# First loads in written order, lora_B behind the last weight block, A in three transfers, and column steps at multiples of 16

## The chip, the cores and the metric

The kernel runs on one core of one Trainium2 chip. The metric is device time in microseconds: the median of three runs is 418.48 us before the change (417.75 to 418.6). Besides these there is one profiled execution, from which all durations in this text come.

## What is computed

For each of 64 batch entries a 64x64 matrix is picked from 16 by an index and applied to x; the result goes through a 1024x1024 layer and a routed rank-8 correction, and is added to x.

```python
W = weights[condition]                                   # one of 16, for each batch entry
c = jnp.einsum('bct,bcd->bdt', x, W).reshape(-1, 1024)   # 4096 rows
top1 = jnp.argmax(c @ gate_w.T + expert_bias, axis=-1)   # one of 4 experts
base = c @ W_up.T
z = jnp.einsum('nh,erh->ner', c, lora_A)                 # rank 8
d = jnp.einsum('ner,ehr->neh', z, lora_B)                # scale 1
out = x + base + (the row d[n, top1[n]])
```

All is float32, and x has 64 x 64 x 1024 elements.

## The kernel before

**Order of the algebra.** The picked matrix acts on the rows of a batch entry and the layer on its columns, so the kernel first multiplies x by one wide matrix (gate, lora_A and W_up side by side: `NW` = 1060 columns), giving `u`, and then applies the picked matrix (`bd`, block diagonal for two batch entries) to `u`. x is cut into 32 tiles of 128 rows, and two tiles form a group `g`. Each float32 operand is split into a high and a low part (`split_a`, `split_b`: ACT copies the rounded value, DVE subtracts it), and each product is three matmuls: high by high, high by low and low by high.

**Blocks.** A group's rows (tile a, tile b) and the contraction (two halves of four 128-row slices, `KH` = 4) give A11, A12, A21, A22; the wide matrix is cut in the same way into B11, B12 (columns 530 to 1059), B21 and B22. Each block of B is loaded in four slices k of 128 x 530 (265 KB) by `load_b`, into temporary buffers of a pool of ten. The first two groups (`eight`) compute all eight block products; the other fourteen (`seven`) compute seven products with sums of blocks, `S1` to `S4` and `T1` to `T4`. A product of 530 columns goes in two PSUM banks of 264 and 266 columns (`BANKS`, `CUT`).

**The start.** For the first group `load_halves` brings A11 and A21 together on ACT's queue, slice k=0 alone and k=1 to 3 in one transfer, and A12 with A22 on SP's. SP's queue also has all slices of B. TensorE's order in group 0 is: A11 and A21 by B11, slice by slice; A12 and A22 by B21; A11 by B12; A21 by B12; A12 by B22; A22 by B22. Small warm-up matmuls (`keep_warm`) stand before and between the first slices.

**What sets the order.** `InOrder` wraps an engine so that its instructions keep the order in which they are written; the lists of hooks (`at`, `each`) put the work of ACT, DVE and the queues behind a given slice of a given product. Loads given to `nc.sync` instead of the wrapped `sync` may be placed by the planner elsewhere in SP's queue. In the kernel before, `load_b`, `load_half`, the first B11 pieces, A12/A22 and lora_B are such loads; the planner put two of lora_B's three transfers (`load_b3`, 32 rows of 4 KB each) ahead of the last slice of B12, and the third behind B22. An SP load that shares a completion counter with the eighth load before it waits for that one to land; some wait for a temporary buffer too.

**ACT's order after the first products**, as far as it matters here: the four slices of B12, the first `bd`, B22's first slice, `u` of tile 0 (`uh`), B22's second, `u` of tile 1, lora_B (`split_b3`), `zt`, B22's last two.

**Columns of y.** Each tile's `u` is applied and written in three steps, `COLS`, of at most 354 columns. The first 36 columns are gate and lora_A, so the steps cover 318, 354 and 352 columns of y. `finish` is one step: `apply` (three matmuls with `bd`), `delta` (one with lora_B), `evict`. The last two tiles are written step by step. Tile 30 (`LAST`) has four steps, and the last product of its group is made one bank after the other (`product_by_bank`).

Of the kernel before, what the change touches and what calls it, by code (L numbers as in the profile page):

```python
# [17 lines left out]
KH = KC // 2  # L18
H = KC * P
E, R = 4, 8  # L20
ER = E * R
# [2 lines left out]
NB = NW // 2  # L24
CUT = 264
LEFT = 512 - CUT
COLS = ((0, 354), (354, 354), (708, 352))
LAST = ((0, 354), (354, NB - 354), (NB, CUT), (NB + CUT, NB - CUT))
WARM = 27
GATE = (("lg", E), ("mx", 1), ("sc", E), ("m2", 1), ("zm", ER))  # L30
HALVES = (slice(0, 64), slice(64, 128))
# [14 lines left out]
def kernel(  # L46
# [53 lines left out]

    def load_half(i, hf):
        t = raw[i, hf] = xp.tile([P, KH, P], F32, name="xh", tag="xh")
        nc.sync.dma_start(t, xt[i, hf])

    def minus_both(t, one, two):
        vector.scalar_tensor_tensor(t, one, -1.0, two, ALU.mult, ALU.subtract)
# [32 lines left out]
    def part(q, k):  # L139
        i, j = int(q[1]) - 1, int(q[2]) - 1  # L140
        return w[j][KH * i + k]

    def load_b(q, k):
        t = raw[q, k] = temp("wraw")
        nc.sync.dma_start(t, part(q, k))  # L145

    def split_b(q, k, n=slice(0, NB)):
        scalar.copy(wh[q][:, k, n], raw[q, k][:, n])
# [58 lines left out]
            )  # L207

    BANKS = slice(0, CUT), slice(CUT, NB)

    def product(g, which, hooks):

# [7 lines left out]

    def product_by_bank(g, places, a, b, hooks):

        for m, (o, n) in enumerate(zip(places, BANKS)):
            for k in range(KH):
                part_of_product(g, a, b, True, k, o[:, : n.stop - n.start], n)
                for kk, fn, *args in hooks:
                    if kk == KH * m + k:
                        fn(*args)
# [61 lines left out]
            vector.tensor_sub(b[p, 1, p], t[p], b[p, 0, p].bitcast(F32))  # L290

    FIRST = NB - G

    def place():
        return psum.tile([P, 512], F32, name="o", tag="o", bufs=2)
# [53 lines left out]
    def evict(i, j):  # L349

        s, d = ycols(i, j)
        o = os_.pop((i, j))[:, s]
        if i == NP - 1 or d.start >= FIRST and i == NP - 2:
            vector.tensor_add(ys[i][:, d], o, ys[i][:, d])
            sync.dma_start(out[i, :, d], ys[i][:, d])
            return
        if i < NP - 2 and j == 0:
            ys[i] = yp.tile([P, H], F32, name="y", tag="y")
        scalar.copy(ys[i][:, d], o)
        if i == NP - 2 and j == 1:  # L360
            n = slice(0, FIRST)
            pool.dma_start(ys[i][:, n], x[i][:, n], accum_op=ALU.add)
        elif j == 2:
            pool.dma_start(ys[i], x[i], accum_op=ALU.add)
            nc.sync.dma_start(out[i], ys.pop(i))
# [25 lines left out]
            raw["x", hf][:, :, k], xt[0:2, hf].rearrange("i p k q -> p i k q")[:, :, k]  # L391
        )

    ONE, REST = slice(0, 1), slice(1, KH)
    load_halves(scalar, 0, ONE)
    load_halves(scalar, 0, REST)

    one = cpool.tile([P, 1], F32, name="one")
    vector.memset(one, 0.0)
# [10 lines left out]
    t = raw["B11", 0] = temp("wraw")  # L410
    pieces = slice(0, CUT), slice(CUT, NB)
    for n in pieces:
        nc.sync.dma_start(t[:, n], part("B11", 0)[:, n])  # L413
    for k in range(1, KH):
        load_b("B11", k)
    load_halves(nc.sync, 1, slice(0, KH))
    for k in range(KH):
        load_b("B21", k)
    split_a(0, "A11", ONE)
    split_b("B11", 0, pieces[0])  # L420
    split_b("B11", 0, pieces[1])
    split_a(0, "A21", ONE)

    row = cpool.tile([P, 1], I32, name="row")
    for p in HALVES:
# [24 lines left out]
    def load_b3():  # L450
        b3f = yp.tile([3 * ER, H], F32, name="b3f", tag="y")
        for a in range(3):
            nc.sync.dma_start(b3f[ER * a : ER * a + ER], lb)
        raw["b3"] = b3f

    def split_b3():
# [19 lines left out]
    def eight(g):  # L476
        a, b = 2 * g, 2 * g + 1
        h = [[] for _ in range(6 if g == 0 else 8)]

        def at(s, k, fn, *args):  # L480
            h[s].append((k, fn, *args))

        def each(s, k, fn, q, ks, *args):
            for i in ks:
                at(s, k, fn, q, i, *args)

        one, two = (0, 1), (2, 3)
        if g == 0:
            each(0, -1, load_b, "B12", range(KH))
            at(0, 0, keep_warm, 6)  # L490
            at(0, 0, split_a, g, "A11", REST)
            at(0, 0, make_idx)
            for i in range(4):
                at(0, 0, load_cond, i)
            each(0, 0, split_b, "B11", (1,))
            at(0, 0, split_a, g, "A21", REST)
            each(0, 0, split_b, "B11", two)
            at(0, 1, keep_warm, 4)
            at(0, 0, split_a, g, "A12")
            each(0, 0, split_b, "B21", (0,))  # L500
            at(0, 1, split_a, g, "A22")
            each(0, 2, split_b, "B21", (1, 2))
            each(0, 3, split_b, "B21", (3,))
            each(1, -1, load_b, "B22", range(KH))
            at(1, 0, load_b3)
            for i in (2, 3):
                at(1, 0, load_half, i, 0)
            each(1, 0, split_b, "B12", (0,))
            each(1, 1, split_b, "B12", (1,))
            each(1, 2, split_b, "B12", two)  # L510
            at(1, 2, split_cond, a)
            at(1, 3, split_cond, b)
            each(1, 3, split_b, "B22", (0,))
            at(2, -1, lambda: u_of(a, 0, c["1"]))
            at(2, 0, load_two, 0)
            at(2, 0, load_two, 1)
            each(2, 0, split_b, "B22", (1,))
            at(2, 2, apply, a, 0)
            at(2, 2, gate, a)
            at(2, 2, lambda: u_of(b, 0, c["2"]))  # L520
            at(2, 3, split_b3)
            at(3, 1, turn, a)
            for i in (2, 3):
                at(3, 0, load_half, i, 1)
            each(3, 1, split_b, "B22", two)
            at(3, 2, split_a, g + 1, "A11")
            at(3, 3, delta, a, 0)
            at(3, 3, evict, a, 0)
            at(4, 1, apply, b, 0)
            at(4, 1, gate, b)  # L530
            at(4, 2, split_a, g + 1, "A21")
            at(5, -1, lambda: u_of(a, 1, c["3"]))
            at(5, 0, turn, b)
            at(5, 0, sum_t1, one)
            at(5, 0, load_two, 2)
            at(5, 0, load_two, 3)
            at(5, 2, delta, b, 0)
            at(5, 2, evict, b, 0)
            at(5, 2, end_t1, one)
            at(5, 3, split_a, g + 1, "A12")  # L540
            at(5, 3, finish, a, 1)
            order = (
                [("1", "A11", "B11", True), ("2", "A21", "B11", True)],
                [("1", "A12", "B21", False), ("2", "A22", "B21", False)],
                ("3", "A11", "B12", True),
                ("1", "A21", "B12", True),
                ("3", "A12", "B22", False),
                ("1", "A22", "B22", False),
            )
        else:  # L550
            p = a - 1
            at(0, -1, lambda: u_of(p, 1, cs[g - 1]["1"]))
            at(0, 1, finish, p - 1, 2)
            at(0, 1, split_a, g, "A22")
            at(0, 2, make_t1, two)
            at(0, 3, finish, p, 1)
            at(1, 0, finish, p, 2)
            at(1, 1, load_cond, a + 2)
            at(1, 1, load_cond, b + 2)
            for i in (b + 2, a + 2):  # L560
                at(1, 1, load_half, i, 0)
                at(2, 1, load_half, i, 1)
            at(2, 1, make_t2, one)
            at(3, -1, lambda: u_of(a, 1, c["1"]))
            at(3, 2, make_t2, two)
            at(4, -1, lambda: u_of(b, 1, c["2"]))
            at(4, 1, sums, g + 1, "S1")
            at(4, 2, split_cond, a)
            at(4, 2, split_cond, b)
            at(5, 0, sums, g + 1, "S2")  # L570
            at(5, 1, split_a, g + 1, "A11")
            at(5, 2, sums, g + 1, "S3")
            at(6, 0, split_a, g + 1, "S2")
            at(7, -1, lambda: u_of(a, 0, c["3"]))
            at(7, 0, sums, g + 1, "S4")
            order = (
                ("1", "A11", "B12", True),
                ("2", "A21", "B12", True),
                ("1", "A12", "B22", False),
                ("2", "A22", "B22", False),  # L580
                ("3", "A11", "B11", True),
                ("1", "A21", "B11", True),
                ("3", "A12", "B21", False),
                ("1", "A22", "B21", False),
            )
        run(g, order, h, c)
        cs[g] = dict(c)


    def seven(g):  # L590
# [6 lines left out]
        def at(s, k, fn, *args):  # L597
            h[s].append((k, fn, *args))
# [115 lines left out]
        if last:  # L714
# [8 lines left out]
            places = place(), place()  # L723

            def u_bank(m):
                n = BANKS[m]
                vector.tensor_add(s[:, n], places[m][:, : n.stop - n.start], ts["t8"][:, n])
                scalar.copy(us[a][0][:, NB + n.start : NB + n.stop], s[:, n])

            def u_bank_low(m):  # L730
                n = BANKS[m]
                u_low(a, slice(NB + n.start, NB + n.stop), s[:, n])

            product_by_bank(
# [8 lines left out]
                    (5, u_bank_low, 0),  # L743
                ],
            )
            sync.dma_start(out[a, :, :FIRST], ys[a][:, :FIRST])
            u_bank(1)
            finish(b, 2, chain()[:, :512])
            u_bank_low(1)
# [52 lines left out]
```

## Time and profile before

| | us |
|---|---|
| median of three runs | 418.48 |
| time of the profiled execution | 422.16 |
| its span, first to last instruction | 420.4 |
| TensorE busy | 410.9 |
| DVE busy | 285.5 |
| ACT busy | 184.6 |
| first matmul of a product | 4.19 |
| last matmul starts | 415.6 |

The page has one line of busy times by engine, a row for each engine in forty slices of the span (10.5 us each, a digit for tenths), the granted clock of TensorE in the same slices, the chain of work that ended last, and groups of like instructions. A line of the timeline has: start, duration, engine, line of the source, operation, output<-inputs, sizes, how many instructions were merged, and in brackets how long the engine stood idle before and what ended that. PE is TensorE, PEld its weight load, DVE the vector engine, ACT the scalar engine, POOL GpSimd, SP the engine that issues most transfers. Line L42 is the wrapper `InOrder`, so almost all instructions have it, and the names of tiles tell them apart: `hB`, `lB` are high and low of the B blocks, `hT`, `lT` those of T1 to T4 (B12 lives in T4's buffer and so shows as `hT`), `ah`, `al` those of A, `wraw` a loaded slice of B, `xx` the first A halves, `b3f` lora_B as loaded, `c` and `o` PSUM.

### The profile page before, as it was taken

The numbers are of one execution on the slowest core, as the hardware profiler recorded it, in microseconds if no ns is written. First come the engines' busy times: TensorE is split into PE (matmuls) and PEld (weight loads), VectorE is DVE, ScalarE is ACT, GpSimd is POOL, SyncE is SP. The second block draws the span as 40 slices with busy tenths as digits, with TensorE's granted clock in tenths as the row PEclk, the third lists the DMA queues.
The fourth block names the chain that finished last, engine by engine and source line by source line (L and its number), as shares of the span: only waits on it lengthen the run. The fifth ranks groups of instructions, "written<-read, shape, count | busy, mean of one in ns | idle before, by whom it ended". The sixth has DMA issues, their size and how long they took to land.

```text
span 420.4 us, 8155 instructions
## 1 busy us (share of the span) xinstructions
PE 410.9 (98%) x3197; PEld 408.7 (97%) x3197; DVE 285.5 (68%) x643; ACT 184.6 (44%) x416; POOL 75.8 (18%) x92
## 2 busy tenths in 40 slices
PE   8979999999999999999999999999999999999995
PEld 7969999999999999999999999999999999999995
DVE  4587784876766767676666757666676676666755
ACT  5564655353434534343353434445334444524531
POOL 6202611202020210202011020201102020020000
PEclk9989999999999999999999999999999999999998
DMA  8966992455654436564354655535464453564435
GB/s 274 317 227 175 225 248 54 111 166 134 175 120 84 132 106 177 133 154 101 95 145 120 175 133 133 123 81 152 127 177 133 102 125 93 165 170 113 90 63 175
DMA packets 25414, 60.99 MB, mean 145 GB/s; under 512 B 3264, under 2 KB 4928, under 8 KB 25376
## 3 DMA queue, kind: packets, MB, share of 16 engines
q1 hardware_dynamic: 18128, 40.74, 27.3%
q0 software_dynamic: 6704, 19.21, 26.9%
q8 instruction: 25, 0.41, 0.4%
q10 hardware_dynamic: 544, 0.52, 0.4%
q14 instruction: 13, 0.11, 0.1%
HBM read 43.68 MB, written 16.78 MB: 144 GB/s over the span
## 4 chain that ended last, share of the span: by engine, by line
PE 93%; DMA 4%; DVE 1%; SPq 0%; issue 0%; ACT 0%; DVEq 0%
PE c L42 77%; PE o L42 16%; DMA wraw<-in_w_dram 2%; DMA xx<-in_xt_dram 2%; SPq L145 0%; SPq L413 0%; DVE bd L42 0%; DVE ul L42 0%; DVE al L42 0%; ACT hT L42 0%; ACT ah L42 0%; DVE lB L42 0%; DVE y L42 0%; DVE lT L42 0%; DVEq L42 0%
## 5 line engine op out<-in xcount | busy, mean ns | idle before, releaser
L42 PE MATMUL c<-hT,ah 128*128 128x264 f32 x480 | 140.7, 293 | 0.0
L42 PE MATMUL c<-lT,ah 128*128 128x264 f32 x480 | 137.9, 287 | 0.0
L42 PE MATMUL c<-hT,al 128*128 128x264 f32 x480 | 137.9, 287 | 0.0
L42 PE MATMUL c<-hB,ah 128*128 128x264 f32 (+1 forms) x424 | 122.1, 288 | 0.6 <-ACT hB L42 0.5
L42 PE MATMUL c<-lB,ah 128*128 128x264 f32 (+1 forms) x424 | 121.0, 285 | 0.4 <-DVE lB L42 0.4
L42 PE MATMUL c<-hB,al 128*128 128x264 f32 (+1 forms) x424 | 121.0, 285 | 0.0
L42 PEld LDWEIGHTS c<-lT,ah 128*128 128x128 f32 x480 | 91.8, 191 | 0.0
L42 PEld LDWEIGHTS c<-hT,al 128*128 128x128 f32 x480 | 91.6, 191 | 0.0
L42 PEld LDWEIGHTS c<-hT,ah 128*128 128x128 f32 x480 | 91.6, 191 | 0.0
L42 POOL DMA_DIRECT2D y<-in_x_dram x31 | 29.8, 960 | 290.2 <-ACT y L42 285.2
L42 PEld LDWEIGHTS c<-lB,ah 128*128 128x128 f32 x424 | 80.5, 190 | 0.7 <-DVE lB L42 0.7
L42 PEld LDWEIGHTS c<-hB,ah 128*128 128x128 f32 x424 | 80.2, 189 | 1.0 <-ACT hB L42 1.0
L42 PEld LDWEIGHTS c<-hB,al 128*128 128x128 f32 x424 | 80.1, 189 | 0.0
L42 ACT COPY y<-o 128x318 f32<-128x318 f32 (+2 forms) x91 | 40.1, 442 | 58.2 <-PE o L42 56.3
L42 ACT CAST uh<-usum 128x530 fp32r<-128x530 f32 (+4 forms) x44 | 27.1, 616 | 69.7 <-DVE usum L42 69.7
L42 DVE TENSOR_TENSOR al<-S,ah 128x512 fp32r<-128x512 f32 x56 | 38.5, 687 | 24.2 <-ACT ah L42 24.2
L42 DVE TENSOR_TENSOR al<-xh,ah 128x512 fp32r<-128x512 f32 x46 | 31.7, 689 | 30.2 <-ACT ah L42 30.2
L42 PE MATMUL o<-uh,bd 128*128 128x354 f32 (+2 forms) x186 | 45.3, 325 | 2.7 <-ACT uh L42 2.7
L42 DVE TENSOR_TENSOR ul<-usum,uh 128x530 fp32r<-128x530 f32 (+4 forms) x44 | 30.0, 682 | 18.6 <-ACT uh L42 18.6
L42 ACT CAST zt<-o 96x128 fp32r<-96x128 f32 x31 | 8.1, 261 | 77.8 <-PE o L42 77.8
L42 POOL DMA_INDIRECT wsel<-in_cw_dram,idx x32 | 35.2, 1101 | 10.5 <-issue 5.2
L42 ACT CAST ah<-S 128x512 fp32r<-128x512 f32 x56 | 34.9, 623 | 1.8 <-DVE S L42 1.4
(87 smaller groups left out, 471.6 us busy)
## 6 DMA issues: line engine op xcount, KB each, us to landing
xh<-in_xt_dram SPq DMA_DIRECT2D x60, 256.0 KB, 5.1
y<-in_x_dram POOLq DMA_DIRECT2D x30, 512.0 KB, 5.7
out_dram<-y SPq DMA_DIRECT2D x30, 512.0 KB, 2.9
wraw<-in_w_dram SPq DMA_DIRECT2D x23, 265.0 KB, 7.2
T<-in_w_dram POOLq DMA_DIRECT2D x8, 265.0 KB, 6.7
xx<-in_xt_dram SPq DMA_DIRECT2D x1, 512.0 KB, 7.2
wsel<-in_cw_dram,idx POOLq DMA_INDIRECT x32, 5.0
y<-in_x_dram SPq DMA_DIRECT2D x1, 512.0 KB, 3.3
```

The lines of the kernel that those rows point to most:

```text
L42: return lambda *a, **k: self.tc.keep_in_program_order(fn(*a, **k))
```

## The change

- `load_b`, the first B11 pieces, A12/A22, lora_B and the x halves of the first four tiles go through the wrapped `sync`, in written order. lora_B's three transfers so stand behind B22.
- A11/A21 come in three transfers: k=0 and k=1 on ACT's queue, k=2 and 3 on SP's between B11's second and third slice. B11's second slice is split in two column pieces (264 and 266), as the first was, and A's splits follow the three transfers.
- Four warm-up matmuls instead of six after the first slice.
- `COLS` and `LAST` have new limits, so that the steps of y have 320, 352 and 352 columns. For tile 30 the last two steps have 258 and 272 instead of 264 and 266, and the banks of the last product follow (`LAST_BANKS`). The stores of tile 30 are cut at column 480 (`STORED`) instead of 494.

```diff
-COLS = ((0, 354), (354, 354), (708, 352))
-LAST = ((0, 354), (354, NB - 354), (NB, CUT), (NB + CUT, NB - CUT))
+COLS = ((0, 356), (356, 352), (708, 352))
+LAST = ((0, 356), (356, NB - 356), (NB, 258), (NB + 258, NB - 258))
...
-        nc.sync.dma_start(t, xt[i, hf])
+        (sync if i < 4 else nc.sync).dma_start(t, xt[i, hf])
...
-        nc.sync.dma_start(t, part(q, k))
+        sync.dma_start(t, part(q, k))
...
+    LAST_BANKS = [slice(c0 - NB, c0 - NB + n) for c0, n in LAST[2:]]
...
+    STORED = FIRST // 16 * 16
...
+            if d.start == FIRST:
+                d = slice(STORED, d.stop)
             sync.dma_start(out[i, :, d], ys[i][:, d])
...
-    ONE, REST = slice(0, 1), slice(1, KH)
-    load_halves(scalar, 0, ONE)
-    load_halves(scalar, 0, REST)
+    STEPS = slice(0, 1), slice(1, 2), slice(2, KH)
+    for k in STEPS[:2]:
+        load_halves(scalar, 0, k)
...
-        nc.sync.dma_start(t[:, n], part("B11", 0)[:, n])
-    for k in range(1, KH):
+        sync.dma_start(t[:, n], part("B11", 0)[:, n])
+    load_b("B11", 1)
+    load_halves(sync, 0, STEPS[2])
+    for k in range(2, KH):
         load_b("B11", k)
-    load_halves(nc.sync, 1, slice(0, KH))
+    load_halves(sync, 1, slice(0, KH))
...
-    split_a(0, "A11", ONE)
-    split_b("B11", 0, pieces[0])
-    split_b("B11", 0, pieces[1])
-    split_a(0, "A21", ONE)
+    def split_first(k):
+        split_a(0, "A11", STEPS[k])
+        for n in pieces:
+            split_b("B11", k, n)
+        split_a(0, "A21", STEPS[k])
+
+    split_first(0)
...
-            nc.sync.dma_start(b3f[ER * a : ER * a + ER], lb)
+            sync.dma_start(b3f[ER * a : ER * a + ER], lb)
...
-            at(0, 0, keep_warm, 6)
-            at(0, 0, split_a, g, "A11", REST)
+            at(0, 0, keep_warm, 4)
+            at(0, 0, split_first, 1)
...
-            each(0, 0, split_b, "B11", (1,))
-            at(0, 0, split_a, g, "A21", REST)
-            each(0, 0, split_b, "B11", two)
+            at(0, 0, split_a, g, "A11", STEPS[2])
+            each(0, 0, split_b, "B11", (2,))
+            at(0, 0, split_a, g, "A21", STEPS[2])
+            each(0, 0, split_b, "B11", (3,))
...
-            sync.dma_start(out[a, :, :FIRST], ys[a][:, :FIRST])
+            sync.dma_start(out[a, :, :STORED], ys[a][:, :STORED])
```

More of the change, by code (lines that the diff above doesn't have):

```diff
@@ L221, in product_by_bank @@
     def product_by_bank(g, places, a, b, hooks):
-        for m, (o, n) in enumerate(zip(places, BANKS)):
+        for m, (o, n) in enumerate(zip(places, LAST_BANKS)):
             for k in range(KH):
@@ L725, in u_bank @@
             def u_bank(m):
-                n = BANKS[m]
+                n = LAST_BANKS[m]
                 vector.tensor_add(s[:, n], places[m][:, : n.stop - n.start], ts["t8"][:, n])
@@ L730, in u_bank_low @@
             def u_bank_low(m):
-                n = BANKS[m]
+                n = LAST_BANKS[m]
                 u_low(a, slice(NB + n.start, NB + n.stop), s[:, n])
```

## The prediction

> **What bounds the kernel now.** I read the busy shares first, then TensorE's timeline, then the chain that ended last, then the stretches of the DMA engines. The first two lines are from the page.
>
> ```profile
> PE 410.9 (98%) x3197; PEld 408.7 (97%) x3197; DVE 285.5 (68%) x643; ACT 184.6 (44%) x416; POOL 75.8 (18%) x92
> ...
> PEclk9989999999999999999999999999999999999998
> ```
>
> TensorE is busy 98% of the span. In its timeline the starts of neighbouring matmuls lie 0.12 us apart, and from 28.4 us on no two lie more than 0.26 us apart until the last ones at 415 us. So nothing that another engine or a transfer does after 28.4 us sets the end; what can be won lies before it and behind 415.9 us, where TensorE stops. Its timeline before 28.4 us, in two pieces:
>
> ```profile
> 7.21 0.39 PE L42 MATMUL c<-hB,ah 128*128 128x264 f32 x1 [0.47 <-ACT hB L42]
> 7.95 0.40 PE L42 MATMUL c<-lB,ah 128*128 128x264 f32 x1 [0.36 <-DVE lB L42]
> ```
>
> ```profile
> 20.65 0.28 PE L42 MATMUL c<-hT,al 128*128 128x266 f32 x1
> 23.61 0.59 PE L42 MATMUL o<-uh,bd 128*128 128x354 f32 x2 [2.67 <-ACT uh L42]
> 24.49 0.43 PE L42 MATMUL o<-ul,bd 128*128 128x354 f32 x1 [0.29 <-DVE ul L42]
> ...
> 25.26 0.43 PE L42 MATMUL c<-hT,ah 128*128 128x266 f32 x1
> 25.48 0.43 PE L42 MATMUL c<-lT,ah 128*128 128x266 f32 x1
> ```
>
> There are two holes. The small one waits for the halves of the second B11 block. The large one stands after the third block of B12 and names ACT's `uh`; the chain that ended last and ACT's timeline tell why `uh` was late:
>
> ```profile
> 3.08 7.24 DMA xx<-in_xt_dram
> ...
> 11.71 9.09 DMA wraw<-in_w_dram
> ```
>
> ```profile
> 20.82 0.63 ACT L42 CAST hT<-wraw 128x530 fp32r<-128x530 f32 x1 [3.82 <-DMA wraw<-in_w_dram]
> ...
> 22.96 0.59 ACT L42 CAST uh<-c 128x530 fp32r<-128x530 f32 x1
> ```
>
> ACT sat in its queue for the fourth block of B12, issued at 11.71 and landed at 20.80 us. SP's timeline has two of lora_B's transfers ahead of it (issued 10.34 and 11.01), and the stretches show what happened to the DMA engines (busy us and matmuls, clock, DMA share, GB/s):
>
> ```profile
> 12.00:13.60 1.60, 1.60 (x15) 1.00 1.08 404
> 13.60:15.60 2.00, 2.00 (x18) 1.00 1.04 211
> 15.60:17.60 2.00, 2.00 (x19) 1.00 1.07 284
> ```
>
> The engines stay full while the rate falls by half for about 4 us. The third block of B12 landed at 16.3, the two pieces of lora_B at 17.5 and 18.3, then came 2.5 us until the fourth block, and after it one B22 block each 0.7 us.
>
> **The change, part by part.**
>
> *lora_B behind B22.* In SP's order the fourth block of B12 moves from behind two lora_B pieces to directly behind the third, and the four B22 blocks move up by two places. An SP load waits for the landing of the eighth transfer before it, so the fourth block may go at about 10.4 us (when A12/A22 has landed) instead of 11.71. At the 0.7 us per block seen after 20.8 it lands near 17, and the first B22 block, which ACT splits ahead of `uh`, near 18. TensorE needs them at 20.8. The hole then closes: from 20.77 (20.65 plus one interval of 0.12) to 24.76, where B12's fourth block starts, is 3.99 us, less the three real `o` matmuls in it at 0.16 each: **3.50 us** saved, if the loads come in before 19.
>
> *What follows the hole.* Of the matmuls from 25.04 to 28.36, fifteen are 0.221 us apart instead of 0.122: 15 x 0.099 = **1.5 us**, at a granted clock of 0.50 between 26 and 28 us. That row against a rule: the Trainium skill (TensorE: Matmul & The Clock Gate, Part 1: The HAM clock gate) says that an idle window of some 3.4 us halves the clock, and that the window runs freely, not from the start of the program. By the row the closed hole returns 1.5 us; by the rule it is a matter of where the windows fall, and an execution in which the hole straddles two windows never paid it, so there is nothing to return. I keep 1.5 for the profiled execution and **0.7** for the median; 0 and 1.5 are the ends.
>
> *A11 and A21 in three transfers.* Columns k=1 (128 KB) now come alone on ACT's queue; k=2 and 3 (256 KB) go to SP behind the second B11 block. That block landed at 6.46 with 384 KB of A beside it; with 256 KB less ahead, at the 0.33 MB/us of these stretches, it lands some 0.75 us sooner. ACT and DVE also split it in two pieces (0.41 and 0.43 us each instead of 0.63 and 0.71), so the first product can start after half of it. The k=1 products start near 6.6 instead of 7.21 and no longer wait 0.75 us for the low half: TensorE gets to the end of the step over a microsecond earlier. But there it meets A12/A22, which landed at 10.32: ACT 0.63, ACT 0.64, DVE 0.71 bring the first low half of B21 to 12.39, and TensorE came for it at 12.77. Only 0.38 us of slack is there, so of the 1.1 us I count **0.35**. Two warm-up matmuls less are inside this. A rule speaks against even that: DMA: Bandwidth & Descriptors, Issuing engines are not separate DMA queues, has all queues run on the same 16 engines, so that moving a transfer from ACT to SP buys nothing but the issue time (and here SP issues one more, 0.43 us). By the rule this part is 0, by the row 0.35; I follow the row, as B11's block really shared the engines with bytes not wanted yet. With A12/A22 landing 0.5 us late it would be -0.15, with it 0.8 sooner 1.1.
>
> *Loads in written order.* Loads of x halves of the first four tiles keep their places; B22's third and fourth wait for their buffers (DVE's low halves of B21, 12.4 and 13.6), as they did. The three lora_B pieces queue behind B22, ahead of the x halves and the reloaded B11/B12, whose places and bytes are unchanged. Queued behind lora_B on ACT: its split (1.05), `zt`, the splits of B22's last two blocks.
>
> *Columns.* 354+354+352 becomes 356+352+352, and 318+354+352 becomes 320+352+352: the same 1060 and 1024 columns, so TensorE's sum is unchanged: **0** for the body. In the last tile 264/266 becomes 258/272: six columns more in each of five last links, 0.03 us. The last stores become 240, 136 and 136 KB. The trace has 176 KB (352 columns, starting at a multiple of 16) landing in 2.4 us, 177 KB (354) in 2.6 and the very last 133 KB in 2.7; so 0 to 0.3 us, taken as **0.1**.
>
> *Sum.* In the profiled execution 3.5 + 1.5 + 0.35 + 0.1 = 5.45: its span goes from 420.4 to 414.95, its time from 422.16 to 416.7. That execution is 3.68 us above the median of the runs, and the page doesn't say where. For the median I take 3.5 + 0.7 + 0.35 + 0.1 = 4.65: **418.48 - 4.65 = 413.8 us**.
>
> **Rivals.** *The excess sits in the hole.* If the 3.68 us are all in the 5.0 us of hole and half clock, the plain runs have 1.3 of it to give, and with the two small terms 1.75: 416.7. For it: the rest of the kernel is paced by TensorE alone. Against: the dip to 211 GB/s is too deep to be the profiler's.
>
> *lora_B is late for the first correction.* The first product with lora_B (`o<-b,zt`) ran at 30.08; 5.35 us sooner is 24.7. Before it stand ACT's split 1.05, DVE's 1.22 and `zt`'s low half 0.3: the last piece must land by 22.1. Its bytes: 5.78 MB up to it in queue order, 4.08 moved by 13.6; 1.4 MB at 0.38 MB/us and the last 0.39 at 0.21 give 19.3, and 2 us from moved to landed, as for B21's last block, 21.3. If it still lands at 24.2, 2.1 us are lost again: 415.9.
>
> *The same, and worse: slower.* lora_B's transfers are the ones beside which the rate fell; now they run beside the x halves and reloads. Each us of landing past 22.1 costs one; the gain is gone at 26.75, and from 27.6 the kernel is slower by over 0.2%. At 28.5 it is 420.2. Against: that is 4 us later than it landed before with the same bytes ahead.
>
> *The dip belongs to the gathers of `wsel`* issued at 7.3 to 12.0, not to lora_B. Then the fourth block gains only the 256 KB, 0.7 us, and the clock stays as it was: with the small terms 1.15, 417.3.
>
> **How the numbers follow.** A change of 0.2% (0.84 us) is about what a measurement of this kernel tells from none. Chances: hole gone and most of its price back 0.59 (412.4 to 415.2), excess in the hole 0.18, lora_B late 0.10, gathers 0.07, slower 0.06. Low end of the range: 3.5 + 1.5 + 0.8 + 0.3 = 6.1, 412.4; high end 417.0, past the second and third case. Faster: 0.59 + 0.18 + 0.10 + a third of the gathers, 0.89; same 0.05; slower 0.06.
>
> **What would show it.** The step from B12's third to fourth block without a gap and ACT's wait for `wraw` before `hT` under 1 us; a granted clock of 1.00 from 24 to 30 us; B12's fourth block landing before 19; the k=1 products starting by 6.7 and B21's first still near 12.3; `o<-b,zt` first at 24.7 and unstalled; the stretch at 211 GB/s moved to about 17 to 20 us; TensorE's end at 410.5. I am wrong if a new hole stands ahead of `o<-b,zt`, if the rate still halves near 14 us, or if B21 waits for A12.

## The result, and the profile after

| us | before | after |
|---|---|---|
| median (16 runs each) | 418.57 | 416.83 |
| lowest to highest | 417.0 to 420.54 | 415.84 to 418.3 |
| profiled execution: time, span | 422.16, 420.4 | 416.98, 415.2 |

The ratio is 0.9946 (95% interval 0.9928 to 0.9964). It is the ratio of the means, and the means differ by 2.26 us, as more of the runs before are late ones. The medians differ by 1.74 us (0.42%), where 4.65 was forecast. For the profiled execution the forecast was 416.7, and 416.98 was measured.

The page of the changed kernel, its busy line and clock row as before:

```profile
PE 410.3 (99%) x3195; PEld 408.5 (98%) x3195; DVE 285.4 (69%) x646; ACT 185.3 (45%) x419; POOL 75.5 (18%) x92
...
PEclk9999999999999999999999999999999999999999
```

TensorE's busy time has hardly moved, and the two slices of the clock row that read 8 now read 9. The chain that ended last, from its start (start, duration, what ran; `x` is how many instructions stand together):

```profile
0.74 2.95 DMA xx<-in_xt_dram
...
4.38 3.27 PE c L43 x12
...
10.53 11.12 PE c L43 x90
21.65 0.49 PE o L43 x3
22.13 2.21 PE c L43 x18
```

From 4.38 us on the chain is TensorE alone. The weight block that stood in the chain before (9.09 us of `wraw`) is gone from it. ACT's timeline shows why:

```profile
13.10 2.83 ACT L43 CAST hT<-wraw 128x530 fp32r<-128x530 f32 x4
...
18.73 0.60 ACT L43 CAST uh<-c 128x530 fp32r<-128x530 f32 x1 [1.20 <-PE c L43]
...
22.80 1.05 ACT L43 CAST b<-b3f 96x1024 fp32r<-96x1024 f32 x1 [2.42 <-DMA b3f<-in_lb_dram]
```

The four blocks of B12 are split in one run with no wait, the fourth done by 15.93 instead of 21.45. ACT is now free for `uh` at 17.53 and waits 1.20 us for TensorE's product, the other way round from before. lora_B's split waits 2.42 us for its data instead. The stretches (busy us and matmuls, clock, DMA share, GB/s) and the two ends of TensorE's steady part:

```profile
13.60:15.60 2.00, 2.00 (x19) 1.00 1.05 378
15.60:17.60 2.00, 2.00 (x19) 1.00 1.10 366
17.60:19.60 2.00, 2.00 (x18) 1.00 1.01 206
19.60:21.60 2.00, 2.00 (x18) 1.00 1.04 308
```

```profile
25.89 0.41 PE L43 MATMUL o<-b,zt 96*128 96x320 f32 x1
...
411.33 0.29 PE L43 MATMUL o<-b,zt 96*128 96x272 f32 x1
```

The dip to about 206 GB/s has moved behind B22 with lora_B. The hole and the half clock after it are gone. In the profiled executions the kernel divides into four parts:

| part of the profiled execution, us | before | after |
|---|---|---|
| start to B12's first product (the front) | 18.57 | 19.27 |
| from there to the first `o<-b,zt` | 11.51 | 6.62 |
| from there to the last matmul's start (the body) | 385.49 | 385.44 |
| from there to the end of the span (the tail) | 4.83 | 3.87 |

So 4.9 us came from the hole and its clock, 0.96 from the tail, and 0.7 was lost in the front. (The third part is nearly the same in these two, but not in the other executions; see cols_only.) The forecast for this execution was met by two errors of opposite sign: it had 0.35 us gained in the front and 0.1 in the tail.

One row already says that the forecast for the median was not sound: of the 219 runs of the kernel before that were timed with this result and the experiments below, one (422.52) was slower than the profiled execution's 422.16. The profile showed an extreme execution. The granted clock says the same of the half clock: of the 18 profiled executions in this text, the three with a stretch at half clock behind the start have a mean clock of 0.992 to 0.994, the fifteen others 0.996 or more; of the 203 runs for which the clock is on record, four are at 0.994 or below.

### The profile page after: what moved, and what is told of

Its sections match the earlier page's. It is cut to its first block, busy times and chain, and to the rows that moved or that the text cites. A ratio compares the mean times of both kernels' runs of the same rounds, so it can differ in the third digit from the quotient of the medians.

```text
span 415.2 us, 8159 instructions
## 1 busy us (share of the span) xinstructions
PE 410.3 (99%) x3195; PEld 408.5 (98%) x3195; DVE 285.4 (69%) x646; ACT 185.3 (45%) x419; POOL 75.5 (18%) x92
## 4 chain that ended last, share of the span: by engine, by line
PE 98%; DMA 1%; ACT 0%; DVE 0%; issue 0%
PE c L43 82%; PE o L43 16%; DMA xx<-in_xt_dram 1%; DVE y L43 0%; ACT hB L43 0%; ACT ah L43 0%
## 5 line engine op out<-in xcount | busy, mean ns | idle before, releaser
L43 PEld LDWEIGHTS c<-hT,al 128*128 128x128 f32 x480 | 90.6, 189 | 0.0
L43 ACT COPY y<-o 128x352 f32<-128x352 f32 (+1 forms) x91 | 40.2, 443 | 57.3 <-PE o L43 55.8
L43 PE MATMUL o<-uh,bd 128*128 128x356 f32 (+2 forms) x186 | 44.8, 322 | 0.0
```

The lines of the kernel that those rows point to most:

```text
L43: return lambda *a, **k: self.tc.keep_in_program_order(fn(*a, **k))
```

## The experiments

The theory put to the test was that of the prediction: the hole is caused by lora_B's place and is in every run. The rivals: the hole is large only in some executions; the gain comes from A's transfers, or from the stores at the end. Experiments of one set ran beside the same runs of the kernel before; the medians of these are 419.08, 418.39, 418.85 and 418.3 us in the four sets, so that times of different sets are compared by what they gain on it. The ratios follow the means of the runs and so count late executions more than the medians do.

### First set: which part of the change pays

**before_again**: the kernel before, unchanged, for a second profile.

> The kernel before, unchanged, to see what other executions of it pay at the hole ahead of B12's fourth slice. Theory 1 (the hole of the first profile is typical, only the half clock comes and goes): the runs fall into two groups about 1.5 us apart, the later one with a mean granted clock near 0.992, the earlier near 1.00; the profile again shows the fourth slice of B12 landing after 20 us and a hole of 3 us or more. Theory 2 (the first profile caught an unusually late landing): the hole is 1 to 2 us, its end before 23.5 us, and the times spread without two groups.

Measured: 419.05 us, ratio 1.0009 (0.9991 to 1.0026). Its profile (418.05 us) has no hole. ACT's wait for the fourth B12 block, which was 3.82 us in the first profile, in its timeline:

```profile
16.64 0.64 ACT L42 CAST hT<-wraw 128x530 fp32r<-128x530 f32 x1 [1.43 <-DMA wraw<-in_w_dram]
```

The block was there at 16.6 instead of 20.8 us, with the same instructions in the same order and the same two lora_B pieces ahead. It was issued at 10.48 instead of 11.71 and took 6.1 instead of 9.1 us. The dip is in this execution too (249 GB/s from 14 to 16 us). TensorE needed what ACT does behind it only at about 21. What follows: the size of the hole is not a property of the code but of the execution. Neither expectation came true as it stood, as both had a hole of 1 us or more.

**lora_only**: the kernel before, with the loads of the start in written order, hence lora_B behind B22. Nothing else.

```diff
-        nc.sync.dma_start(t, part(q, k))
+        sync.dma_start(t, part(q, k))
...
-            nc.sync.dma_start(b3f[ER * a : ER * a + ER], lb)
+            sync.dma_start(b3f[ER * a : ER * a + ER], lb)
```

> The kernel before with its first loads in written order, so that lora_B stands behind B22; A in two transfers and the columns as before. Theory 1 (the whole gain is lora_B's place, A12 limits the front): 1.5 to 2.0 us faster than before, as the full change. Theory 2 (the three transfers of A or the columns carry part): 1 us or less.

Measured: 417.79 us, ratio 0.9979 (0.996 to 0.9997). No hole; the fourth block split at 16.16. A gain, but of about 0.9 us (1.3 by the medians) rather than 4.2; this is the second expectation by the ratio, and between the two by the medians.

**lora_first**: the changed kernel, with two lora_B pieces ahead of B12's fourth block again.

```diff
-            each(0, -1, load_b, "B12", range(KH))
+            each(0, -1, load_b, "B12", range(KH - 1))
+            at(0, -1, load_b3, (0, 1))
+            at(0, -1, load_b, "B12", KH - 1)
...
-            at(1, 0, load_b3)
+            at(1, 0, load_b3, (2,))
```

> The changed kernel with two of lora_B's transfers again ahead of B12's fourth slice; all else as changed. Theory 1 (only lora_B's place counts): within 0.3 us of the kernel before, a hole before B12's fourth slice, the rate falling to some 200 GB/s near 14 us. Theory 2 (the gathers of the picked matrices make the dip): about 0.7 us slower than the changed kernel and no deep dip at 14 us.

Measured: 417.72 us, ratio 0.9958 (0.9942 to 0.9974). In its profile the dip is back where it was, and a small hole with it (B12's first product to `o<-b,zt` is 7.87 us, against 6.6 without a hole). The stretch of the dip, of lora_first and then of lora_only:

```profile
14.00:16.00 2.00, 2.00 (x18) 1.00 1.04 200
```

```profile
14.00:16.00 2.00, 2.00 (x18) 1.00 1.07 369
...
18.00:20.00 2.00, 2.00 (x19) 1.00 0.97 229
```

So the dip follows lora_B and not the `wsel` gathers, which kept their place: that rival falls. The first expectation was right about the dip and wrong about its price: the time is not that of the kernel before but 1.4 us below its median, where the changed kernel is 1.7 to 1.8 below.

**two_A**: the changed kernel with A11 and A21 in two transfers as before, six warm-ups, and B11's second slice split in one piece.

```diff
-    STEPS = slice(0, 1), slice(1, 2), slice(2, KH)
+    STEPS = slice(0, 1), slice(1, KH)
...
-    load_halves(sync, 0, STEPS[2])
...
-            at(0, 0, keep_warm, 4)
-            at(0, 0, split_first, 1)
+            at(0, 0, keep_warm, 6)
+            at(0, 0, split_a, g, "A11", STEPS[1])
...
+            each(0, 0, split_b, "B11", (1,))
+            at(0, 0, split_a, g, "A21", STEPS[1])
+            each(0, 0, split_b, "B11", two)
```

> The changed kernel with A11 and A21 in two transfers, both on ACT's queue, B11's second slice split in one piece and six warm-up matmuls, as before. Theory 1 (A12's landing or the cold clock set the end of the front): within 0.4 us of the changed kernel. Theory 2 (with the hole gone, TensorE passes its front on to the end, one for one): 0.7 to 1.2 us slower than the changed kernel.

Measured: 416.64 us, ratio 0.9959 (0.9939 to 0.9979). Most runs are as good as those of the changed kernel, but 6 of 22 lie at 419.2 to 420.3; the changed kernel has none above 418.3 in 34 runs. So what two_A undoes doesn't move the usual execution; it seems to take away a late one. In all kernels here that have this part together with lora_B behind B22, 1 of 104 runs is above 418.3.

### Second set: the tail, and the late executions

**cols_only**: the kernel before with the new column steps and stores only.

```diff
-COLS = ((0, 354), (354, 354), (708, 352))
-LAST = ((0, 354), (354, NB - 354), (NB, CUT), (NB + CUT, NB - CUT))
+COLS = ((0, 356), (356, 352), (708, 352))
+LAST = ((0, 356), (356, NB - 356), (NB, 258), (NB + 258, NB - 258))
...
+    STORED = FIRST // 16 * 16
...
```

> The kernel before with only the columns changed: steps of 320, 352 and 352, last cuts at 258 and 272, stores cut at column 480. Theory 1 (a store whose rows start or end inside a 64-byte line is confirmed late): from the last matmul to the end of the span 3.85 us instead of 4.8, and 0.9 us faster than the kernel before, whatever the front does. Theory 2 (the prediction's term, landing times of the stores): 0.1 us, at most 0.3.

Measured: 417.28 us, ratio 0.9972 (0.9958 to 0.9986). Its tail is 3.89 us. Its body, from the first `o<-b,zt` to the last, is shorter too; TensorE's timeline of before_again, then of cols_only:

```profile
25.65 0.41 PE L42 MATMUL o<-b,zt 96*128 96x318 f32 x1
...
411.37 0.29 PE L42 MATMUL o<-b,zt 96*128 96x266 f32 x1
```

```profile
25.39 0.41 PE L42 MATMUL o<-b,zt 96*128 96x320 f32 x1
...
410.81 0.29 PE L42 MATMUL o<-b,zt 96*128 96x272 f32 x1
```

That is 385.72 us against 385.42. Over all profiles, the bodies with the old columns take 385.65 to 385.72 us (385.49 in the very first profile), those with the new ones 385.37 to 385.44, but for after_warm31 with its half clock: 0.27 us less. Why is not known. The part that the prediction took at 0.1 gives 1.1 us of the median (418.39 to 417.28), the largest single share, and tail and body (0.79 and 0.27) add up to it.

**cut_750**: the changed kernel with the last cut of tile 30 two columns lower, at column 750 of y (byte 3000 of a row) instead of 752 (3008). Before the change it was 758 (3032).

```diff
-LAST = ((0, 356), (356, NB - 356), (NB, 258), (NB + 258, NB - 258))
+LAST = ((0, 356), (356, NB - 356), (NB, 256), (NB + 256, NB - 256))
```

> The changed kernel with the last two steps of tile 30 cut two columns earlier: 256 and 274 columns, so that the last two stores meet at column 750 of y (byte 3000), not at 752 (byte 3008, a multiple of 64). Theory 1 (the line boundary): the end of the span again 4.7 to 4.9 us behind the last matmul, 0.9 us slower than the changed kernel. Theory 2 (the sizes of the last steps or stores, 256/274 beside 258/272): within 0.1 us of the changed kernel.

Measured: 417.52 us, ratio 0.9966 (0.9951 to 0.998). Its tail is 4.44 us. SP's waits near the end (sum, count, longest) say where; in this order before_again, cut_750, and the changed kernel in a later profile:

```profile
SPq L796 <- DMA out_dram<-y: 2.4, 1, 2.4
```

```profile
SPq L807 <- DMA out_dram<-y: 1.9, 2, 1.0
```

```profile
SPq L807 <- DMA out_dram<-y: 1.3, 2, 0.7
```

Two columns cost 0.57 us of tail in this one profile, with the same bytes to within 1 KB. The runs agree in sign: the median gains 0.9 us here and 1.7 to 1.8 in the changed kernel, though the intervals of the ratios overlap. So size alone doesn't decide; where the boundary between two stores falls in memory bears on it. The tail lies between the two expectations (4.7 to 4.9, and that of the changed kernel). As each row ends at byte 4096, a last store that starts at a multiple of 64 also has rows of a multiple of 64 bytes; the two can't be told apart here.

**two_A_warm**: two_A with 16 warm-ups in place of 6 behind the first slice. If the late executions come from a clock that stays half because TensorE stood idle there, more warm-ups remove them.

```diff
-            at(0, 0, keep_warm, 6)
+            at(0, 0, keep_warm, 16)
```

> The kernel with A11 and A21 in two transfers, lora_B behind B22 and the new columns, with sixteen warm-up matmuls instead of six ahead of B11's second slice. Theory 1 (its late executions, 6 of 22 above 419 us, are those whose clock opens a window later because TensorE waits 1 us for that slice): none or one of some 20 above 419 us, the lower ones at 416.4 as before. Theory 2 (the late ones come from late landings): the same share of late executions, a quarter.

Measured: 417.17 us, ratio 0.9966 (0.9952 to 0.998), and again 6 of 22 are late, though less so (418.5 to 419.0). The profile is of a late one (418.72 us); TensorE's timeline, then DVE's:

```profile
7.18 0.42 PE L43 MATMUL c<-hB,al 128*128 128x266 f32 x1
7.40 1.93 PE L43 MATMUL o<-warm 128*128 128x128 bf16 x16
...
9.40 0.59 PE L43 MATMUL c<-hB,ah 128*128 128x264 f32 x1
10.43 0.39 PE L43 MATMUL c<-lB,ah 128*128 128x264 f32 x1 [0.44 <-DVE lB L43]
10.65 0.28 PE L43 MATMUL c<-hB,al 128*128 128x264 f32 x1
```

```profile
9.51 0.25 DVE L43 TENSOR_SCALAR idx<-o,rowf 128x32 int32<-128x32 f32 x1 [2.83 <-PE o L43]
9.67 0.70 DVE L43 TENSOR_TENSOR lB<-wraw,hB 128x530 fp32r<-128x530 f32 x1
```

Up to about 10.3 us the products are 0.22 us apart (durations of 0.42), later 0.12 (0.28): the clock opened late. The clock column reads 1.00 for such stretches, so that only the intervals show it. B12's first product stands at 21.01 where the other two_A profile has 18.75.

This run doesn't settle whether idleness is to blame, as its own warm-ups hold the front back: at half clock sixteen take 1.93 us, and the high half of B11's second slice was ready (ACT split it from 6.40 to 7.03) when they began. DVE's two lines show more. With A in two transfers DVE computes `idx`, an index that waits for a small TensorE matmul behind the warm-ups, and only then that slice's low half. Here it waited 2.83 us, and the low half came late. The change also turned this order round, as its diff has `split_first` ahead of `make_idx`; DVE in the changed kernel, whose clock opened late too:

```profile
6.54 0.78 DVE L43 TENSOR_TENSOR lB<-wraw,hB 128x264 fp32r<-128x264 f32 x2 [0.99 <-ACT hB L43]
...
8.27 0.25 DVE L43 TENSOR_SCALAR idx<-o,rowf 128x32 int32<-128x32 f32 x1 [0.75 <-PE o L43]
```

From this slice's first product to the next one it is 0.23 to 0.42 us in all seven profiles with the new order. With the old it is 1.03 us in nine of eleven, 0.84 in before_look2 and 0.75 in the first profile of all. No run separates the order from the division of A.

**before_look**: the kernel before, one more profile.

> The kernel before, unchanged, one more profile, to see an execution above 420 us (a third of them are). Theory 1 (late clock): in such a one the clock opens at 9 us or later, and there is no hole ahead of B12's fourth slice. Theory 2 (late landing): the fourth slice lands after 19 us and TensorE stands still ahead of it for 2 us or more. If the execution is below 419.5 us: neither.

Measured: 418.28 us, a hole and clock of 0.85 us together, the fourth block at 18.18.

### Third set: is it the clock at the start?

The number of warm-ups ahead of the first product (`WARM`, 27) is what could move the opening of the clock.

**after_again**: the changed kernel, unchanged.

> The changed kernel, unchanged, beside the next three. Theory (three small gains add: columns 1.1, A's three transfers 0.6, lora_B's place 0.5): 0.5% faster than the kernel before, no execution above 419 us. Its profile: the fourth slice of B12 split before 17 us, no hole; B21's first product near 12.1 us if the clock opened before 6.5 us, near 13.4 if at 9 us.

Measured: 417.07 us, ratio 0.9954 (0.9938 to 0.9969). In its profile (416.37 us) the clock opened at 4.0 instead of 9.1 us, and B12 began at 18.68. B21's first product came at 12.05, as expected, and the next one 0.75 us later, for want of the low half of B21's first slice. This is the place at which the prediction put the limit of this part. ACT had waited 1.00 us for A12 and A22 there, but then 0.60 us more before it split that slice (in after_warm31 the profile names the slice's own transfer).

**after_warm31**: the changed kernel with `WARM = 31`.

> The changed kernel with 31 warm-up matmuls at the start instead of 27, so that they end at about 4.2 us, when the first product can begin, and not at 3.85. Theory 1 (whether the clock opens early hangs on the idle stretch of 0.3 to 0.6 us ahead of the first product): the clock opens before 8 us in its profile, and the slower half of the executions moves down: median 0.2 to 0.5 us below the changed kernel. Theory 2 (it hangs only on where the window falls): no change, or 0.1 us slower for the later start.

Measured: 416.94 us, ratio 0.9956 (0.9943 to 0.9969): no difference to the changed kernel, as the second expectation had it. But one run in 21 is at 419.98, and the profile is of that one. ACT's and TensorE's timelines and the stretches:

```profile
24.76 1.05 ACT L43 CAST b<-b3f 96x1024 fp32r<-96x1024 f32 x1 [2.83 <-DMA b3f<-in_lb_dram]
```

```profile
25.41 0.28 PE L43 MATMUL c<-hT,al 128*128 128x266 f32 x1
27.42 0.42 PE L43 MATMUL o<-b,zt 96*128 96x320 f32 x1 [1.74 <-DVE zt L43]
```

```profile
27.90:31.10 3.20, 3.20 (x16) 0.50 0.67 254
```

lora_B landed at 24.7, TensorE stood from 25.5 to 27.4 for `zt`, and the clock then fell to half. This is the rival "lora_B is late for the first correction", in one execution of nine profiled ones with lora_B behind B22.

**after_cold** and **before_cold**: the changed kernel and the kernel before, each with `WARM = 4`, so that the clock should open late in nearly all runs.

> The changed kernel with four warm-up matmuls at the start instead of 27[...]. Theory (a late clock costs the changed kernel what TensorE then lacks at B21): clock opening at 8 to 11 us, one group of times, about 1.3 us above the lowest ones of the changed kernel (417.2 to 418.5). If the front were hidden behind A12's landing: within 0.3 us of the changed kernel.

> The kernel before with four warm-up matmuls at the start instead of 27. Theory 1 (its late third, 420.0 to 421 us, are executions with a late clock): nearly all of its executions at 420 us or above, one group. Theory 2 (the late third comes from late landings of B12): the times stay in two groups, the lower one at 418 to 419.

Measured: after_cold 417.34 us, ratio 0.9949 (0.9931 to 0.9966); before_cold 419.24 us, ratio 1.0005 (0.9983 to 1.0028). In both the first expectation missed and the other came out. The clock did open late (10.4 and 12.9 us in the profiles, B12's first product at 19.86 and 21.58), yet after_cold's median is within 0.3 us of the changed kernel's, and before_cold has only 4 of 14 runs above 420, the others being a group at 418.6 to 419.4. What can be said of the kernel before is that its quickest runs were lost (lowest 418.62 instead of 416.85). A clock that opens late is therefore at most a part of the late executions and not the explanation of them.

### Fourth set: the remaining edit, and more profiles

**stored_494**: the changed kernel with tile 30's first store cut at column 494 again (byte 1976).

```diff
-    STORED = FIRST // 16 * 16
+    STORED = FIRST
```

> The changed kernel with the stores of tile 30 cut at column 494 again (byte 1976, inside a 64-byte line), the last cut staying at 752. Theory 1 (only the boundary of the last two stores counts): from the last matmul to the end of the span 3.85 us, and the time of the changed kernel. Theory 2 (each boundary inside a line costs its share, as 4.45 us with one and 4.8 with two boundaries suggest): about 4.2 to 4.45 us, 0.4 to 0.6 us slower than the changed kernel.

Measured: 416.81 us, ratio 0.9962 (0.9949 to 0.9975), tail 3.88. This cut does nothing that can be measured; the stores it bounds are issued 0.7 us or more ahead of the last one (411.30 and 412.01). Only the cut at 752 counts.

**before_look2**, **before_look3**, **before_look4**: the kernel before, three more profiles.

> The kernel before, unchanged: one more profile for the size of the hole ahead of B12's fourth slice. Theory 1 (the hole of the first profile was a rare one): the slice is split by ACT before 18.5 us and TensorE loses less than 1 us to it. Theory 2 (it is ordinary): after 20 us, 2 us or more. At 420 us or above: a clock that opens at 9 us or later.

> As the look before: Theory 1 the slice split before 18.5 us and less than 1 us lost; Theory 2 after 20 us and 2 us or more. At 420 us or above: a clock that opens at 9 us or later.

> As the two looks before: Theory 1 the slice split before 18.5 us and less than 1 us lost; Theory 2 after 20 us and 2 us or more. At 420 us or above: a clock that opens at 9 us or later.

Measured: 420.23, 419.14 and 418.01 us, each late in its own way. before_look3 has a hole of 2.0 us; its fourth block in ACT's timeline:

```profile
19.50 0.64 ACT L42 CAST hT<-wraw 128x530 fp32r<-128x530 f32 x1 [2.80 <-DMA wraw<-in_w_dram]
```

before_look4 has one of 0.16 us, and waits 0.4 us more for `zt`. before_look2, the slowest, has none. There the second transfer of A11 landed 2.5 us later than in the first profile, ACT's timeline and TensorE's:

```profile
7.65 0.51 ACT L42 CAST ah<-xx 128x384 fp32r<-128x384 f32 x1 [2.86 <-DMA xx<-in_xt_dram]
```

```profile
8.75 0.39 PE L42 MATMUL c<-hB,ah 128*128 128x264 f32 x1 [1.85 <-ACT hB L42]
```

```profile
10.70:14.00 3.30, 3.30 (x19) 0.50 1.02 363
```

TensorE stood 1.85 us for the second slice and 0.45 us soon after, and from 10.7 us the clock was at half for 3.4 us. That transfer of 384 KB (k=1 to 3 in one) is the one that the change divides.

### All profiles in one table

"Interval" is the time from B12's first product to the first `o<-b,zt`: 6.6 us with no hole, and what is above it is hole, wait and half clock. "Tail" is from the start of the last matmul to the end of the span.

| profile | lora_B | A | B12 starts | interval | tail |
|---|---|---|---|---|---|
| before | ahead | 2 | 18.57 | 11.51 | 4.83 |
| before_again | ahead | 2 | 19.07 | 6.58 | 4.93 |
| before_look | ahead | 2 | 18.58 | 7.44 | 4.79 |
| before_look2 | ahead | 2 | 21.74 | 6.58 | 4.39 |
| before_look3 | ahead | 2 | 18.77 | 8.57 | 4.30 |
| before_look4 | ahead | 2 | 18.62 | 7.25 | 4.68 |
| before_cold | ahead | 2 | 21.58 | 6.59 | 5.05 |
| cols_only | ahead | 2 | 18.81 | 6.58 | 3.89 |
| lora_first | ahead | 3 | 17.97 | 7.87 | 3.87 |
| lora_only | behind | 2 | 18.70 | 6.59 | 4.70 |
| two_A | behind | 2 | 18.75 | 6.58 | 4.27 |
| two_A_warm | behind | 2 | 21.01 | 6.59 | 3.89 |
| cut_750 | behind | 3 | 18.93 | 6.62 | 4.44 |
| stored_494 | behind | 3 | 19.23 | 6.62 | 3.88 |
| after | behind | 3 | 19.27 | 6.62 | 3.87 |
| after_again | behind | 3 | 18.68 | 6.63 | 3.87 |
| after_cold | behind | 3 | 19.86 | 6.62 | 3.91 |
| after_warm31 | behind | 3 | 18.79 | 8.63 | 3.85 |

With lora_B ahead the nine intervals are above 6.6 by a median of 0.65 us and at most 4.9; with lora_B behind eight of nine are at 6.6. With A in two transfers three of eleven fronts are late, at 21.0 to 21.7; with three, none of seven is later than 19.9, though the clock opened after 9 us in three of them. Of the three late fronts one is a cold start and one has the sixteen warm-ups; only before_look2's is that of an unaltered start. The tail is 4.71 us on average with the cut at 758 (eight profiles, 4.30 to 5.05) and 3.92 with the cut at 752 (nine, 3.85 to 4.27).

## Why the prediction was wrong

**The mechanism held for the profiled execution.** lora_B's pieces set the dip, the fourth block of B12, behind them in the queue, came late, and ACT, standing in its queue for that block, kept `uh` from TensorE. In the changed kernel the fourth block landed before 19, B12 ran without a gap, the clock was 1.00 from 24 to 30 us, and the dip moved to 17.6 to 19.6. All of these were named beforehand.

**The step that failed** is "The hole then closes: [...] **3.50 us** saved", carried into the sum for the median, with 0.7 of half clock beside it. For the profiled execution the pair, 5.0 us, measured 4.9. For the median it measured 0.65 us as the median of nine profiles with lora_B ahead; in the runs, 0.2% (lora_only) or 0.13% (two_A against cols_only), that is 0.9 or 0.6 us (1.3 us by lora_only's medians). So 4.2 us was put where something near 1 belonged. The half clock beside it has no part in the median: by the clocks of the runs it seems to be in about 4 of 203. The prediction saw that its execution was 3.68 us above the median and said that the page did not say where; it then put only 0.8 of it in the disputed place and the rest nowhere in particular. The rival "the excess sits in the hole" did what those numbers asked for and came to 416.7; measured 416.83. Its argument is shown by the second profile of the kernel before; that its time came so close is in part luck, as of the two small terms it added the tail's was far too small.

**Columns: 0 for the body, 0.1 for the tail.** Both were mis-sized, 1.1 us in the runs of cols_only: the tail gave 0.79 us over the profiles, and the body 0.27, though TensorE's columns are as many as before. (The pair of profiles compared first, 385.49 and 385.44, doesn't show the second.) The estimate compared stores of 176 and 177 KB that ran beside one another and beside others; the row to look at was the last store alone, 133 KB in 2.7 us, slower than the 247 KB one in 2.3. In the changed kernel the last two, of 136 KB each, land in 1.8.

**A11 and A21 in three transfers: 0.35.** Measured 0.14% in the runs (lora_first against cols_only, 0.6 us) and 0.05 to 0.13% (two_A against the changed kernel), with intervals that overlap. The size was near, for another reason. There is a limit at B21, as the prediction said (the 0.75 us in after_again), though what ended the wait there was B21's own slice; the usual execution gains nothing. What is gained is that a late front is less late: with the cold start B12 began at 19.86 in the changed kernel and at 21.58 in the kernel before, one profile each, and the clock opened later in the second. Some 0.6 us of it is the order in DVE's queue (1.03 us from the slice's first product to the next, against 0.39), of which the prediction's term had nothing. In the profile that it read, DVE waited for the slice itself (0.16 us, for ACT's half of it); in the others with that order DVE stands at `idx` first. The forecast of the k=1 products near 6.6 held where the clock opened early (6.74 in after_warm31); in the changed kernel's own profile the clock opened at 9.1, and they came at 8.16. The rule that the prediction weighed against the row, by which a transfer moved to another queue buys nothing, agrees with the usual execution; it doesn't speak of the late one.

**The half clock** after the hole: the two answers weighed were 1.5 by the row and nothing by the rule. Both occur, and a wait well under the rule's 3.4 us (the Trainium skill, TensorE: Matmul & The Clock Gate, Part 1: The HAM clock gate) can be enough. It followed the 3.5 us hole, the 2 us wait in after_warm31 and that in before_look2, and it did not follow the hole of 2.0 us in before_look3, whose excess of 1.97 us is the hole alone.

**lora_B late for the first correction**: its split waited 2.42 us and was done at 23.85, in time. In after_warm31 it was late, and 2.0 us went. The slower form of this rival did not occur.

**Sum.** By the ratios, columns 0.28%, A 0.14% and lora_B's place 0.13%, each the difference between two kernels that differ in it, add to 0.55% or 2.3 us; the whole measured 0.54 and 0.46%. Only the first of the three is clear of the noise by itself: each ratio is known to 0.14 to 0.2% either way. lora_only, whose interval (0.03 to 0.40%) just leaves out zero, is the best single evidence for lora_B's place.

**What stays open.** Why the fourth B12 block is split anywhere between 16.6 and 20.8 us in executions of one kernel is not known; it is issued between 10.5 and 11.9 us in all six profiles, so most of the spread lies in its way from there. Of the 219 runs of the kernel before, 59 are at 420 us or more, a group of their own (four runs lie between 419.6 and 420.0); the profiles show three different causes in one late execution each (the hole, A11 late, the clock late with the cold start), and how the 59 divide among them is not settled. Nor is it why a cold start cost the changed kernel so little.

## What to carry to other kernels

A wait seen in one profile of a start that transfers pace is the wait of that execution: take two or three profiles, and where the profiled time is above all timed runs, take the excess off the largest hole first. Order loads so that those which slow the others down stand behind those the first products need; divide the early ones so that one late transfer holds back one slice only; and look in each engine's queue for work that waits for TensorE and stands ahead of work that TensorE will need. Where the last stores split a row, try a cut at a multiple of 64 bytes; here it was the cheapest edit and the largest share of the gain.

## What the runs showed of the hardware

- A boundary between two stores at byte 3008 of a row gave a tail of 3.9 us on average (3.85 to 4.27, nine profiles); at byte 3000 4.44 (one) and at 3032 4.71 (4.30 to 5.05, eight). 3008 is a multiple of 64, the others of 8 only. Which block size decides was not tried.
- While lora_B's 32-row pieces are under way the rate of all queues together falls to 200 to 250 GB/s from about 370 to 400 (before, before_again, lora_first, lora_only, after), wherever in the queue they stand. Whether it is their shape was not tried.
- With 27 warm-ups TensorE's clock opened anywhere from 3.9 to 10.3 us after the start in these profiles (in the two of the changed kernel itself at 4.0 and 9.1), and the clock column reads 1.00 throughout; only the interval between matmuls (0.22 or 0.12 us) tells.
